# A two-layer sequence model on one core: the first MLP's down projection for sequence 1 by a seven-product scheme, gate and up results in one place, less filler beside the values

## The chip, the cores and the metric

The kernel runs on one core of one Trainium2 chip. The metric is device microseconds of that core for one execution. In this text PE is the matrix engine, DVE the vector engine, ACT the scalar engine, POOL the general engine (GpSimd), and SP the engine whose queue issues nearly all DMAs. Each engine works off its own instructions in order and waits for the others by semaphores.

## The reference, cut to what matters

Two sequences of 1024 tokens with 512 features pass through two layers. Each layer is `x = x + attention(layernorm(x))` and then `x = x + mlp(layernorm(x))`. Everything is 32-bit floating point.

- Layer 0: a gated delta rule (a recurrence with 6 heads of 64), and then MLP 0, with 4096 hidden units, whose weights come as 4-bit codes with scales:

```python
gate = jnp.einsum('td,nd->tn', xt, Wg)
up   = jnp.einsum('td,nd->tn', xt, Wu)
inter = gelu_tanh(gate) * up
out  = jnp.einsum('tn,hn->th', inter, Wd)
```

- Layer 1: attention with 16 heads through a small latent (scores by a softmax over 1024 keys, then the values), and then MLP 1, with 2048 hidden units, in which of every four neighbouring hidden units the two largest are kept.

## The kernel before, in words

**The order of the work.** Before a stage in the middle begins, sequence 0 has gone through layer 0, and MLP 0's weights have been unpacked once and kept in HBM (`kept`). This text is about the stage that follows. Two generators run in it, woven together by `weave` (L158): the main one, `first()` (L1873), is layer 1's attention for sequence 0 (`Latent.run`, L1243) and then its norms; the filler, `Second.run` (L1148), is MLP 0 for sequence 1. Each main step yields the microseconds of filler that it wants beside it, each filler step yields what it is worth, and `weave` adds up and takes filler steps until the debt is paid. So the two lists are written out once, in Python, and the order of PE, DVE and ACT is exactly the program's order (`manual_schedule`, L1862). The order of POOL and of SP's queue is set by the framework's planner from its own idea of durations.

**The main one.** After a stage that makes the keys (14 steps), each half of the queries has a score stage and a value stage. A score step (L1335) has 4 short matmuls on separate row groups of PE and two DVE maxima over 128x1024 (L1349); every eighth step POOL also turns a query (L1232, L1233), which PE then transposes (L1240). In the first score stage `Factors.make` (L1678) uses POOL, DVE and SP as well, to prepare sums of MLP 1's weights. A value step (L1393) has 4 matmuls `st_ps` (L1398), two exponentials of 128x1024 on ACT (L1408), 4 matmuls `av_ps` (L1416); each second one has 4 POOL additions of neighbouring exponentials (`pair`, L1430), and the matmuls `den_ps` (L1437) over the sums that POOL made two steps earlier. The kernel gives 3.4 as the wish of both kinds of step (`per_score`, `per_value`).

**The filler.** MLP 0 for sequence 1 goes over 8 chunks `c` of 512 hidden units. A chunk has two pairs of 2x128 units, and each pair a gate and an up product, in all four "units". A unit is a 256 x 512 by 512 x 1024 product that is done by Strassen's scheme in Winograd's form: seven products of half sizes (table `SEVEN`, L212) instead of eight, with sums of the weights before them (`left_sums`, L223, four POOL operations on 128x256, L226 to L229, over tile `z_raw` that a DMA loads), sums of the tokens (`right_sums`, L233, four DVE operations on 128x1024, once, by `tokens`, L948), and sums behind them. The products take turns on two PSUM banks in the order 1, 2, 6, 5, 7, 3, 4; ACT copies three of them out (`part`, L969), DVE adds the copy and the bank (L1014 in `gate`, L1029 in `up`), ACT applies the GELU to the gate's result `g`, and POOL multiplies (L1030) into `h`. One product is a step of 1.7 (`STEP / 2`), two matmuls with 512 columns.

The down projection of a chunk (L1168 to L1176) is plain: for each of 8 token tiles, four matmuls of 512 columns into `o_ps` (issued at L202), one DVE addition into the tile's `x` (L1173), and a step of 3.4. In the last chunk the tile is stored to HBM at once (L1175). The chunk's weights `wd` (1 MB) are loaded at its start (L1154).

A matmul of 32-bit operands is two records in the profile, so a chunk's down projection is 64 records.

**Elsewhere.** `Sevens` (L1716), at the end of the kernel, is MLP 1 for sequence 1; it has its down projection (L1747) by seven products already, with matmuls of 256 columns (L1758), and shares `gate`, `up`, `part` and `step` with `Second`.

Of the kernel before, what the change touches and what calls it, by code (L numbers as in the profile page):

```python
# [27 lines left out]
F32 = mybir.dt.float32  # L28
# [9 lines left out]
P = 128  # L38
B, T, DM = 2, 1024, 512
# [193 lines left out]
def right_sums(eng, b, new):  # L233

    t2, t3, t4 = new[-3:]
    t1 = new[0] if len(new) == 4 else b["12"]
    if len(new) == 3:
        eng.tensor_sub(t3, b["22"], b["12"])
    eng.tensor_sub(t1, b["12"], b["11"])
    eng.tensor_sub(t2, b["22"], t1)  # L240
    if len(new) == 4:
        eng.tensor_sub(t3, b["22"], b["12"])
    eng.tensor_sub(t4, b["21"], t2)
    return {"11": b["11"], "21": b["21"], "22": b["22"], "T1": t1, "T2": t2, "T3": t3, "T4": t4}
# [695 lines left out]
class Seven:  # L940
# [7 lines left out]
    def tokens(self, xT, pool, eng):  # L948

        half = T // 2  # L950
        blocks = {
            f"{i + 1}{j + 1}": xT[:, 2 * i : 2 * i + 2, j * half : (j + 1) * half] for i in range(2) for j in range(2)
        }
        self.right = right_sums(eng, blocks, [pool.tile([P, 2, half], F32, name=f"xt{i}") for i in range(1, 5)])
# [63 lines left out]
    def up(self, left, g, h):  # L1018
# [3 lines left out]
        for p, ps in self.units(left):  # L1022
            if p in (1, 6, 5):
                parts[p] = self.part(ps)
            elif p == 4:
                nc.vector.tensor_mul(h[:, 1, 0], g[:, 1, 0], ps)
            else:
                i, j, other = {2: (0, 0, 1), 7: (1, 1, 5), 3: (0, 1, 6)}[p]
                nc.vector.tensor_add(h[:, i, j], ps, parts[other])  # L1029
                self.soon.append(lambda v=h[:, i, j], w=g[:, i, j]: self.multiplier.tensor_mul(v, v, w))  # L1030
            yield p

# [93 lines left out]
class Second(Seven):  # L1126
# [3 lines left out]
    def __init__(self, core, banks, xT, kept, park):  # L1130
        super().__init__(core, banks, AF.Gelu_apprx_tanh, core.nc.gpsimd)
        self.kept, self.park = kept, park
# [14 lines left out]

    def run(self):  # L1148
# [3 lines left out]
        for c in range(NC0):  # L1152
            wd = self.wp.tile([P, 4, DM], F32, tag="wd", name="wd")
            nc.sync.dma_start(out=wd, in_=self.kept[2][c])  # L1154
            hs = []
            for pair in range(2):
                g = self.tmp.tile([P, 2, 2, T // 2], F32, tag="g", name="g")
                h = self.wp.tile([P, 2, 2, T // 2], F32, tag=f"h{pair}", name="h0")
                hs.append(h.rearrange("p j m t -> p j (m t)"))
                for w in ("gate", "up"):  # L1160
# [4 lines left out]
                    for p in self.gate(left, g) if w == "gate" else self.up(left, g, h):  # L1165
                        self.step(p, 0)
                        yield STEP / 2
            for t in range(TT):  # L1168
                n = TT + t
                tok = slice(t * P, (t + 1) * P)  # L1170
                po = self.banks.one("o_ps")
                product(nc, po, [(hs[j // 2][:, j % 2, tok], wd[:, j, :]) for j in range(4)])
                nc.vector.tensor_add(core.x[n], core.x[n], po)  # L1173
                if c + 1 == NC0:
                    nc.sync.dma_start(out=self.park[n], in_=core.x[n])  # L1175
                yield STEP  # L1176
# [539 lines left out]
class Sevens(Seven):  # L1716
# [30 lines left out]
    def down(self, c, right, n):  # L1747

        nc = self.core.nc
        dm = DM // 2  # L1750
        for q in range(2):
            self.need((c, q))
            left = self.left[c, q]

            def multiply(ps, l, r, first):
                for i in range(2):
                    for k in range(2):
                        nc.tensor.matmul(  # L1758
                            ps[:, i * dm : (i + 1) * dm],
                            left[l][:, k, i * P : (i + 1) * P],  # L1760
                            right[r][k],
                            start=(first and i == 0 and k == 0),
                            stop=(k == 1),
                            skip_group_check=True,
                        )

            at = [[self.x[:, 4 * m + 2 * q : 4 * m + 2 * q + 2, v * dm : (v + 1) * dm] for v in range(2)] for m in range(2)]
            parts = {}
            for p, ps in self.products(multiply):
                if p in (1, 6, 5):  # L1770
# [207 lines left out]
```

## Time and profile before

| | us |
|---|---|
| median of 3 timed runs (lowest to highest) | 3300.68 (3300.08 to 3304.23) |
| the profiled execution's own time | 3295.47 |
| its span, from the first to the last instruction | 3293.4 |
| PE busy in the span | 3171.5 (96%) |
| DVE busy | 1674.2 (51%) |
| ACT busy | 870.6 (26%) |
| POOL busy | 801.1 (24%) |

Busy time of PE is modelled at its ends, since matmuls are pipelined: the distance from one matmul's start to the next one's is the safer measure of what it costs. A matmul's mean duration (some 0.6 us for 512 columns) is its latency, not its distance. "Idle before" in a row is the time in which an engine had nothing running before the instruction, with the event that ended it. The stage in question goes from 1333 us to 2285 us of the span: the key stage begins it, then come scores (from 1418), values (1600), scores (1790), values (1970), and from 2195 the output projection and the norms. The eight down projections begin at 1410, 1517, 1638, 1775, 1899, 2000, 2136 and 2251 us.

### The profile page before, as it was taken

How to read it: one execution, taken by the hardware profiler on the slowest of the kernel's cores; microseconds unless marked ns; L12 is line 12 of the kernel's file. 1: busy time of each engine (PE TensorE's matmuls, PEld its weight loads, DVE VectorE, ACT ScalarE, POOL GpSimd, SP SyncE). 2: the span in 40 equal slices, each digit the busy share in tenths (PEclk: the TensorE clock that was granted, in tenths of full speed). 3: DMA queues.
4: the chain of work that ended last, by engine and by line, in shares of the span. 5: the costliest groups of instructions: out<-in, count | busy, mean ns of one | idle time of the engine just before them, and what ended most of it. 6: DMA issues, size and time to landing. Idle time of an engine off the chain costs nothing.

```text
span 3293.4 us, 34780 instructions
## 1 busy us (share of the span) xinstructions
PE 3171.5 (96%) x12916; PEld 1567.7 (48%) x12916; DVE 1674.2 (51%) x3317; ACT 870.6 (26%) x1224; POOL 801.1 (24%) x870
## 2 busy tenths in 40 slices
PE   7999899999999999998999999999999999999998
PEld 5777754555555554533333333334433233324547
DVE  6887752445544542456222562123575267433766
ACT  4544311111111110210444113621212610342221
POOL 3433102111111101245545114531100810360000
PEclk9999899999999999999999999999999999999999
DMA  2111234222222212245101100014000010005211
GB/s 88 34 28 30 63 93 139 76 77 71 83 59 70 78 47 93 81 144 173 64 20 35 55 33 26 26 48 135 29 26 13 1 61 10 13 25 169 79 45 48
DMA packets 208201, 204.96 MB, mean 62 GB/s; under 512 B 52960, under 2 KB 172256, under 8 KB 206624
## 3 DMA queue, kind: packets, MB, share of 16 engines
q1 hardware_dynamic: 206592, 197.94, 19.6%
q10 hardware_dynamic: 1440, 4.80, 0.4%
q8 instruction: 102, 1.67, 0.2%
q14 instruction: 67, 0.55, 0.1%
HBM read 141.57 MB, written 61.08 MB: 62 GB/s over the span
## 4 chain that ended last, share of the span: by engine, by line
PE 84%; DVE 8%; ACT 2%; DMA 2%; POOL 2%; issue 1%; SPq 1%; DVEq 0%; POOLq 0%; ACTq 0%
PE o_ps L202 18%; PE z_ps L996 16%; PE u_ps L202 10%; PE g_ps L202 10%; PE st_ps L1398 4%; PE s_ps L1340 4%; PE av_ps L1416 3%; PE z_ps L1758 3%; PE den_ps L1437 2%; PE proj_ps L202 2%; DVE cv L463 1%; PE out_ps L202 1%; PE wide_ps L634 1%; DVE rd L1450 1%; PE small_ps L624 1%
## 5 line engine op out<-in xcount | busy, mean ns | idle before, releaser
L1430 POOL TENSOR_TENSOR es<-es 128x512 f32<-128x512 f32 x256 | 317.9, 1271 | 273.1 <-ACT es L1408 203.8
L1349 DVE TENSOR_REDUCE top<-s_ps 128x2 f32<-128x1024 f32 x256 | 301.2, 1218 | 71.4 <-PE s_ps L1340 71.1
L1408 ACT ACTIVATE es<-st_ps 128x1024 f32<-128x1024 f32 x256 | 248.5, 1021 | 240.8 <-PE st_ps L1398 235.4
L202 PE MATMUL o_ps<-wd,h 128*128 128x512 f32 x512 | 236.8, 605 | 2.0 <-POOL h L1030 2.0
L202 PE MATMUL g_ps<-xT,w_gate 128*128 128x512 f32 x512 | 233.1, 597 | 1.3 <-DVE h L935 1.3
L202 PE MATMUL u_ps<-xT,w_up 128*128 128x512 f32 x512 | 232.1, 596 | 1.8 <-ACT gelu L930 1.8
L202 PE MATMUL o_ps<-w_down,h 128*128 128x512 f32 x512 | 228.6, 597 | 0.7 <-DVE h L935 0.5
L969 ACT COPY part<-z_ps 128x512 f32<-128x512 f32 x168 | 98.1, 584 | 453.1 <-PE z_ps L996 354.5
L1398 PE MATMUL st_ps<-q,kT 17*128 17x512 f32 x1024 | 174.5, 640 | 4.2 <-ACT es L1408 1.1
L935 DVE TENSOR_TENSOR h<-gelu,u_ps 128x512 f32<-128x512 f32 x64 | 44.0, 687 | 249.0 <-PE u_ps L202 249.0
L1340 PE MATMUL s_ps<-kT,q 16*128 16x512 f32 x1024 | 153.1, 643 | 3.9 <-DVE top L1349 3.9
L202 PEld LDWEIGHTS o_ps<-wd,h 128*128 128x128 f32 x512 | 92.7, 191 | 134.6 <-issue 126.4
L202 PEld LDWEIGHTS u_ps<-xT,w_up 128*128 128x128 f32 x512 | 94.6, 190 | 109.8 <-issue 104.3
L202 PEld LDWEIGHTS o_ps<-w_down,h 128*128 128x128 f32 x512 | 94.6, 190 | 109.4 <-issue 105.0
L202 PEld LDWEIGHTS g_ps<-xT,w_gate 128*128 128x128 f32 x512 | 94.1, 190 | 107.7 <-issue 103.6
L202 PE MATMUL proj_ps<-xT,wqkv 128*128 128x256 f32 x576 | 132.9, 385 | 11.3 <-ACT gw L421 10.1
L1173 DVE TENSOR_TENSOR x<-x,o_ps 128x512 f32<-128x512 f32 x64 | 44.0, 687 | 193.4 <-PE o_ps L202 193.4
L930 ACT ACTIVATE gelu<-g_ps 128x512 f32<-128x512 f32 x64 | 38.2, 597 | 388.4 <-PE g_ps L202 369.4
L1416 PE MATMUL av_ps<-es,v 128*32 128x512 f32 x1024 | 136.3, 604 | 0.0
L996 PE MATMUL z_ps<-xt,z_raw 128*128 128x512 f32 x256 | 122.2, 600 | 0.0
L202 PEld LDWEIGHTS proj_ps<-xT,wqkv 128*128 128x128 f32 x576 | 107.5, 191 | 29.2 <-ACT gw L421 12.3
L996 PE MATMUL z_ps<-xt,z_sum 128*128 128x512 f32 x256 | 119.5, 601 | 0.8 <-DVE g L1014 0.8
(279 smaller groups left out, 5081.3 us busy)
## 6 DMA issues: line engine op xcount, KB each, us to landing
sums<-factor SPq DMA_DIRECT2D x24, 512.0 KB, 3.1
kept_gate<-w_gate SPq DMA_DIRECT2D x16, 512.0 KB, 3.5
kept_up<-w_up SPq DMA_DIRECT2D x16, 512.0 KB, 3.5
kept_down<-w_down SPq DMA_DIRECT2D x16, 512.0 KB, 3.1
z_raw<-kept_gate SPq DMA_DIRECT2D x16, 512.0 KB, 3.7
z_raw<-kept_up SPq DMA_DIRECT2D x16, 512.0 KB, 3.7
wd<-kept_down SPq DMA_DIRECT2D x8, 1024.0 KB, 4.8
xl<-park SPq DMA_DIRECT2D x32, 256.0 KB, 2.8
```

Source lines behind the costliest of these rows:

```text
L202: nc.tensor.matmul(ps, lhsT, rhs, start=(i == 0), stop=(i == len(pairs) - 1))
L935: nc.vector.tensor_mul(h, gl, pu)
L969: self.core.nc.scalar.copy(t, src)
L996: self.core.nc.tensor.matmul(ps, left[l][:, k, :], self.right[r][:, k, :], start=(first and k == 0), stop=(k == 1), skip_group_check=True,)
L1340: nc.tensor.matmul(tiles[h4 // 2][:, h4 % 2 * 512 : h4 % 2 * 512 + 512], q1s[t][r : r + HALF, gr, :], kT[r : r + HALF, gr, j * 512 : (j + ...
L1349: nc.vector.tensor_reduce(top[:, j, h : h + 2], tiles[e].rearrange("p (i k) -> p i k", i=2), AX.X, ALU.max, negate=True)
L1398: nc.tensor.matmul(tiles[h4 // 2][:, h4 % 2 * 512 : h4 % 2 * 512 + 512], kT[r : r + CR, gr, kt * P : (kt + 1) * P], q2[r : r + CR, gr, :], ...
L1408: nc.scalar.activation(t.rearrange("p i q -> p (i q)"), tiles[e], AF.Exp, scale=HALF**-0.5)
L1416: nc.tensor.matmul(av[gr][32 * h4 : 32 * h4 + 32, :], v[:, kt, 4 * gr + h4, :], es[u][h4 // 2][:, h4 % 2, :], start=(kt == 0), stop=(kt == ...
L1430: nc.gpsimd.tensor_add(t, t, es[u][h4 // 2][:, h4 % 2, :])
L1437: nc.tensor.matmul(den[gr][32 * h4 : 32 * h4 + 32, :], self.ones, es[u - 1][h4 // 2][:, h4 % 2, :], start=(kt == 1), stop=(kt == TT - 1),)
L1758: nc.tensor.matmul(ps[:, i * dm : (i + 1) * dm], left[l][:, k, i * P : (i + 1) * P], right[r][k], start=(first and i == 0 and k == 0), sto ...
```

## The change

- `Second`'s down projection is done by the seven products too. `down_weights` loads `wd` and makes its four sums on POOL, on 128x512 each. Token halves are the row blocks; the tokens are taken in two parts `q`, each of 2 x 256 tokens. For each part DVE makes four sums of the hidden results (`left`, on 128x512), which are issued behind product 1; product 6 is the first to use them. A product is 4 matmuls of 256 columns. ACT copies products 1, 6 and 5 out, DVE adds products 2, 7, 3 and 4 from PSUM into `x`, and POOL adds the three copies into `x`. One product is a step of 1.7.
- The last chunk's stores of `x` all stand behind its last product.
- Gate and up share one place: the gate's result is written where the hidden result will be, the up result stays in the tile `part`, and POOL (in `Sevens`, DVE) multiplies in place. The tile `g` is gone; a `part` is held until that multiplication.
- The sums of the tokens, of `Second` and of `Sevens`, overwrite one block of `xT`, and the sum T3 is made ahead of T1 and T2 instead of behind them.
- `x` of sequence 1 is one tile with 8 slices instead of 8 tiles.
- `per_value` of this stage's attention is 3.0 instead of 3.4.
- `Sevens` calls the same function for its down projection (`output`), with DVE as before.

```diff
 def right_sums(eng, b, new):
-    t2, t3, t4 = new[-3:]
-    t1 = new[0] if len(new) == 4 else b["12"]
-    if len(new) == 3:
-        eng.tensor_sub(t3, b["22"], b["12"])
-    eng.tensor_sub(t1, b["12"], b["11"])
-    eng.tensor_sub(t2, b["22"], t1)
-    if len(new) == 4:
-        eng.tensor_sub(t3, b["22"], b["12"])
+    t2, t3, t4 = new
+    eng.tensor_sub(t3, b["22"], b["12"])
+    eng.tensor_sub(b["12"], b["12"], b["11"])
+    eng.tensor_sub(t2, b["22"], b["12"])
     eng.tensor_sub(t4, b["21"], t2)
...
-    def up(self, left, g, h):
+    def up(self, left, g):
...
             elif p == 4:
-                nc.vector.tensor_mul(h[:, 1, 0], g[:, 1, 0], ps)
+                nc.vector.tensor_mul(g[:, 1, 0], g[:, 1, 0], ps)
             else:
                 i, j, other = {2: (0, 0, 1), 7: (1, 1, 5), 3: (0, 1, 6)}[p]
-                nc.vector.tensor_add(h[:, i, j], ps, parts[other])
-                self.soon.append(lambda v=h[:, i, j], w=g[:, i, j]: self.multiplier.tensor_mul(v, v, w))
+                v = parts[other]
+                nc.vector.tensor_add(v, ps, v)
+                self.soon.append(lambda w=g[:, i, j], v=v: self.multiplier.tensor_mul(w, w, v))
             yield p
+
+    def output(self, left, right, at, adder):
+        nc, dm = self.core.nc, DM // 2
+        def multiply(ps, l, r, first):
+            for i in range(2):
+                for k in range(2):
+                    nc.tensor.matmul(
+                        ps[:, i * dm : (i + 1) * dm],
+                        left[l][:, k, i * P : (i + 1) * P],
+                        right[r][k],
+                        start=(first and i == 0 and k == 0),
+                        stop=(k == 1),
+                        skip_group_check=True,
+                    )
+        parts = {}
+        for p, ps in self.products(multiply):
+            if p in (1, 6, 5):
+                parts[p] = self.part(ps).rearrange("p (i d) -> p i d", i=2)
+            else:
+                x = {2: at[0][0], 7: at[1][1], 3: at[0][1], 4: at[1][0]}[p]
+                nc.vector.tensor_add(x, x, ps.rearrange("p (i d) -> p i d", i=2))
+                if p != 4:
+                    self.soon.append(lambda x=x, v=parts[{2: 1, 7: 5, 3: 6}[p]]: adder.tensor_add(x, x, v))
+            yield p
...
 class Second(Seven):
+    def down_weights(self, c):
+        wd = self.wp.tile([P, 4, DM], F32, tag="wd", name="wd")
+        self.core.nc.sync.dma_start(out=wd, in_=self.kept[2][c])
+        half = DM // 2
+        blocks = {
+            f"{i + 1}{j + 1}": wd[:, 2 * i : 2 * i + 2, j * half : (j + 1) * half] for i in range(2) for j in range(2)
+        }
+        new = [self.wp.tile([P, 2, half], F32, name=f"wd_t{i}") for i in range(2, 5)]
+        right = right_sums(self.core.nc.gpsimd, blocks, new)
+        return {name: [t[:, k, :] for k in range(2)] for name, t in right.items()}
+
+    def left(self, hs, q, calls):
+        blocks = {
+            f"{i + 1}{j + 1}": hs[j][:, :, i, q * HB : (q + 1) * HB] for i in range(2) for j in range(2)
+        }
+        new = [self.wp.tile([P, 2, HB], F32, name=f"h_s{i}") for i in (1, 2, 4)]
+        return left_sums(Recorder(self.core.nc.vector, calls), blocks, new)
 
     def run(self):
...
-            wd = self.wp.tile([P, 4, DM], F32, tag="wd", name="wd")
-            nc.sync.dma_start(out=wd, in_=self.kept[2][c])
+            right = self.down_weights(c)
...
-                g = self.tmp.tile([P, 2, 2, T // 2], F32, tag="g", name="g")
-                h = self.wp.tile([P, 2, 2, T // 2], F32, tag=f"h{pair}", name="h0")
-                hs.append(h.rearrange("p j m t -> p j (m t)"))
+                g = self.wp.tile([P, 2, 2, T // 2], F32, tag=f"h{pair}", name="h0")
+                hs.append(g)
...
-            for t in range(TT):
-                n = TT + t
-                tok = slice(t * P, (t + 1) * P)
-                po = self.banks.one("o_ps")
-                product(nc, po, [(hs[j // 2][:, j % 2, tok], wd[:, j, :]) for j in range(4)])
-                nc.vector.tensor_add(core.x[n], core.x[n], po)
-                if c + 1 == NC0:
+            calls = deque()
+            lefts = [self.left(hs, 0, calls)]
+            for q in range(2):
+                for p in self.output(lefts[q], right, self.places(self.x, q), nc.gpsimd):
+                    self.step(p, 0)
+                    if q == 0 and p == 1:
+                        while calls:
+                            calls.popleft()()
+                    if q == 0 and p == 4:
+                        lefts.append(self.left(hs, 1, calls))
+                    if q == 1 and p == 1:
+                        while calls:
+                            calls.popleft()()
+                    yield STEP / 2
+            if c + 1 == NC0:
+                self.step(4, 0)
+                for n in range(TT, NT):
                     nc.sync.dma_start(out=self.park[n], in_=core.x[n])
-                yield STEP
...
-            yield from att.run(0, "right", parks[0], parks[1], 3.4, 3.4, False, beside=factors.make)
+            yield from att.run(0, "right", parks[0], parks[1], 3.4, 3.0, False, beside=factors.make)
```

## The prediction

> **What bounds the kernel now.** I read the page's busy times first, then the busy time of each engine by stage of the stretch in question, then who made PE wait there, then single rows in order of time. By stage (columns: us of the stretch, then PE, PE's weight loads, DVE, ACT, POOL busy with their counts, granted clock, DMA share, GB/s):
>
> ```profile
> 1340.00:1418.00 78.00, 78.00 (x281) 41.25 (x279) 30.24 (x70) 24.12 (x42) 31.06 (x48) 1.00 0.22 65
> 1418.00:1600.00 182.00, 171.33 (x584) 67.17 (x584) 112.53 (x136) 23.02 (x40) 79.95 (x109) 0.97 0.48 159
> 1600.00:1790.00 190.00, 187.88 (x849) 62.45 (x848) 40.70 (x58) 100.56 (x110) 105.26 (x97) 1.00 0.07 23
> 1790.00:1970.00 180.00, 180.00 (x617) 68.99 (x615) 104.07 (x116) 24.07 (x39) 32.09 (x40) 1.00 0.13 44
> 1970.00:2165.00 195.00, 193.27 (x837) 66.44 (x836) 45.69 (x66) 88.76 (x100) 101.04 (x95) 1.00 0.08 25
> 2165.00:2285.00 120.00, 120.00 (x370) 51.13 (x369) 37.97 (x74) 26.55 (x38) 25.27 (x28) 1.00 0.35 113
> ```
>
> PE is without a gap in four of six stages; DVE is at most 62% busy, ACT 53%, POOL 55%. The whole stretch has two PE waits over 1 us, both in the first score stage:
>
> ```profile
> PE hT_ps L1240 <- POOL n L1233: 8.7, 1, 8.7
> PE o_ps L202 <- POOL h L1030: 2.0, 1, 2.0
> ```
>
> Both are POOL being late, held by a weight load before it in its queue. So PE's own work sets the time here: what it sheds is gained, except where another engine begins to hold it. POOL is the one that has done so.
>
> **What PE sheds.** The price is the distance of starts (PE rows in time, at the stretch's end and in MLP 1's down projection, which has the new form):
>
> ```profile
> 2250.61 3.60 PE L202 MATMUL o_ps<-wd,h 128*128 128x512 f32 x8
> 2254.04 0.60 PE L150 MATMUL ln_ps<-ident,ln_xn 128*128 128x128 f32 x4
> ...
> 3208.89 3.62 PE L1758 MATMUL z_ps<-z_right,z_h 128*128 128x256 f32 x16
> 3212.35 3.62 PE L1758 MATMUL z_ps<-z_right,z_hsum 128*128 128x256 f32 x16
> 3215.80 1.89 PE L1758 MATMUL z_ps<-z_right,z_h 128*128 128x256 f32 x8
> 3217.53 1.89 PE L1758 MATMUL z_ps<-z_right,z_hsum 128*128 128x256 f32 x8
> 3223.21 2.07 PE L1758 MATMUL z_ps<-z_right,z_h 128*128 128x256 f32 x4 [3.79 <-DVE x_last L1774]
> ```
>
> Eight records of 512 columns take 3.43 us (0.429 each); sixteen of 256 take 3.46, or 3.45 (0.216 each). A chunk had 8 token tiles x 3.43 = 27.4 us and gets 14 products x 1.73 = 24.2. Eight chunks: 8 x 3.2 = **26 us less** on the path. PE's changes between main work and filler stay: there are as many main steps as before.
>
> **The lists stay matched.** The main one's wishes were 176 x 3.4 = 598.4 (99 steps at `per_score` or norms, 77 at `per_value`), the filler's worth 8 x (28 x 1.7 + 8 x 3.4) = 598.4. Now it is 99 x 3.4 + 77 x 3.0 = 567.6 against 8 x 42 x 1.7 = 571.2: two products are left over at the end and run alone. So less filler beside the values costs nothing by itself, and a shortage of filler isn't to be expected.
>
> **What is added, and its cover.**
>
> 1. DVE: 8 sums per chunk at 0.69 (as the addition of 128x512 from SBUF, L1777, 0.686), 5.5 us per chunk of over 100; the 8 additions of 0.687 into `x` were there before. In a score step PE takes 4.7 us, and DVE 2.4 for the maxima and some 0.8 for additions; four sums in a row (2.75) are absorbed in two steps. They stand behind a POOL multiplication (L1030); behind the sums on DVE stand product 2's addition and the next maxima. Product 6 needs the second sum some 3 to 6 us after issue. From 0 to 1 us per chunk; I take 0, since the old form needed the same multiplication at once and lost 2.0 us in all.
> 2. ACT: 6 copies of 0.584 per chunk, where it had only exponentials. In a value step it idles 4 us during a down projection. 0.
> 3. The two banks now turn over every 1.73 us, not 3.43. The units run that way already, with no PE wait beyond those above. In MLP 1 the new form lost the 3.79 us above behind DVE, which there also compares hidden units. Between 0 and 112 x 0.07 = 8 us (3.8 us over 56 products there); I take 1, nearer the units.
> 4. POOL, per chunk: 4 sums of `wd` at 1.27 (L1430's shape) and 6 additions into `x` at 1.27: 12.7 us. In the value stages that is 55% going to some 70%. As a total it is covered; by moments see below.
> 5. T3 first, at the start: product 6 began at 1336.41, right behind T2's end, so T2 later by one operation costs 1.2 us:
>
> ```profile
> 1333.78 1.22 DVE L239 TENSOR_TENSOR xt<-xT 128x1024 f32<-128x1024 f32 x1
> 1335.04 1.23 DVE L240 TENSOR_TENSOR xt<-xT,xt 128x1024 f32<-128x1024 f32 x1
> ```
>
>    In `Sevens` the first product waits for a DMA and the order is hidden.
> 6. The last stores: all behind the last product. SP issues them in order (0.33 each) and the next attention's loads after; the first load lands some 6.5 us after the last product (1.3 addition, 2.4 issues, 2.8 landing). DVE then measures it and must have it ready for a transpose about 10.3 us after (three matmul groups of 3.43). 0 to 4; I take 1.
> 7. One place for gate and up: as many operations, other operands: 0. A `part` is held until POOL's multiplication; with 4 buffers ACT would wait only if POOL were over 8 us late.
>
> **Filler beside the values.** 70 value steps now take 210 / 1.7 = 123.5 products, so some 16 steps have one product instead of two: PE needs 6.56 - 1.81 = 4.75 us with `den_ps` and 3.9 without. ACT in a gate unit beside values (rows in time):
>
> ```profile
> 1706.09 1.94 ACT L1408 ACTIVATE es<-st_ps 128x1024 f32<-128x1024 f32 x2
> 1708.05 1.28 ACT L1011 ACT_TABLE_LOAD   x1
> 1709.34 0.60 ACT L1011 ACTIVATE g<-z_ps 128x512 f32<-128x512 f32 x1
> 1709.83 0.62 ACT L1015 ACTIVATE g<-g 128x512 f32<-128x512 f32 x1
> ```
>
> With the second table load ACT needs 1.94 + 2.56 + 0.63 = 5.1 us per step. A third of the filler is gate units, so 5 steps lack 0.4 to 1.2 us: 0 to 6 us; I take 1, since ACT catches up in the next steps.
>
> The skill speaks against such steps. The Trainium skill, "ScalarE: Activation LUTs", section "What ACT_TABLE_LOAD costs", puts every switch of tables at some 2.66 us, 1.28 for the load and 1.38 for a drain. By that an ACT step would be an estimated 7.9 us, over even the old two-product step, and the five steps would lose some 18 us. The row shows the load of 1.28 with the activation beginning 0.01 behind it, so the trace decides for 5.1.
>
> **POOL by moments.** At each chunk's start but the first, POOL meets the four sums of `wd` (5.1 us), whose load can only begin near the end of the chunk before and takes 4.8, and then a `z_sum` group (2.9). That is up to 12.8 us in which the main one's POOL work may be queued behind. A value step's additions have this slack:
>
> ```profile
> 1707.19 5.06 POOL L1430 TENSOR_TENSOR es<-es 128x512 f32<-128x512 f32 x4 [8.60 <-ACT es L1408]
> 1717.76 1.04 PE L1437 MATMUL den_ps<-es,ones 128*32 128x512 f32 x8
> ```
>
> 1717.76 - 1712.25 = 5.5 us. So a start beside values (three of them, by the wishes) costs 0 to 12.8 - 5.5 = 7.3, and a start beside scores (four) costs 0 to the 8.7 that a late turned query cost. Bounds 0 to 57. I take 4 in all: the planner mostly puts work whose input is there first, and twenty-odd waits of POOL for `z_raw` cost PE 10.7. Below nothing: those 10.7 may go, since everything shifts.
>
> **Sum.** -26 + 1 (banks) + 1.2 (T2) + 1 (stores) + 1 (ACT) + 4 (POOL) = **-18 us**. Of the profiled execution: span 3293.4 to 3275, own time 3295.5 to 3277.5. The median of the timed runs is 5.2 above that execution; from 3300.7 I forecast **3283**.
>
> **Rivals.**
>
> - **Nothing new waits**, and the old POOL waits shrink: -26 - 5 + 1 gives 3271. For it: no gap on PE in the second score stage, 45% of POOL free. Against: POOL did hold PE once.
> - **Half is given back on the banks and in DVE.** Copies, sums and maxima meet, and a product of 1.73 us is a short cover: 8 us (item 3) + 8 x 1 (item 1) leaves -26 + 16 = -10: 3291. For it: the 3.79 above. Against: there DVE adds the copies too, and here POOL does.
> - **POOL takes PE's place: slower.** At each of the seven later starts the additions or the query wait behind `wd`'s load and sums. From 33 us on, 4.7 per start, the kernel is slower by over 0.2%; at the bounds, 57 us, it ends at 3300.7 - 26 + 57 = 3332. I put the case at 3312. For it: in-order POOL, 8.7 us once; after that wait the granted clock dipped as well (0.97 in the stage). Against: the load lands some 3 us into the chunk, and slack is 5.5.
> - **The scheme does nothing here**, because the smaller matmuls cost as much: excluded by 0.216 against 0.429, unless weight loads (0.19 each) show up between main steps. 3300, little chance.
>
> **Chances.** Forecast (3277 to 3290) 0.46; nothing waits 0.24; half given back 0.16; POOL slower 0.09; nothing gained 0.05. A measurement here tells 0.2% (6.6 us) from no change. Half of the "half" case lies over 3294.1. Faster by more: 0.46 + 0.24 + 0.08 = 0.78; within: 0.08 + 0.05 = 0.13; slower: 0.09. The range leaves out the slower case and the best tail: 3267 to 3299.
>
> **What would show it.** Right: rows of L202 `o_ps<-wd` gone, 896 records of 256 columns at a distance of 0.216; PE's waits in the stretch under 20 us; the stretch some 18 us shorter, all else alike. POOL wrong: `den_ps` or `hT_ps` waiting for POOL with several us each at chunk starts. Banks wrong: PE waiting for ACT `part` or DVE `x` in the new products. ACT wrong: `st_ps` waiting for `es` in gate units. The prediction fails if one cause comes back at most starts.

## The result and the profile after

The changed kernel takes 3293.3 us (median of 22 runs, 3284.5 to 3302.4), where the kernel before took 3300.8 beside it (22 runs, 3292.1 to 3309.5): a ratio of 0.9979, with a 95% interval of 0.9969 to 0.9989, or 7.5 us less. The forecast was 3283, 18 less. Two executions that ran much longer at a lower granted clock, one of `e16_all_three` (4051.9 us) and one of the kernel before in the last round (3397.4 us), are left out of the medians and ratios in this text. Its profiled execution took 3296.5, with a span of 3294.8.

The stage in question is measured below from the first product of `Second` to the first gate-score matmul of MLP 1 behind it. It took 948.6 us before and 947.3 after. By stage, in the columns of the prediction's table (keys, scores, values, scores, values, output and norms; line numbers are now those of the changed kernel):

```profile
1338.00:1416.00 78.00, 78.00 (x296) 44.29 (x295) 33.38 (x76) 26.39 (x46) 32.50 (x49) 1.00 0.22 65
1416.00:1617.00 201.00, 180.73 (x681) 89.71 (x680) 126.89 (x150) 30.18 (x52) 109.56 (x133) 0.93 0.45 144
1617.00:1798.00 181.00, 177.16 (x896) 71.75 (x895) 47.53 (x68) 94.21 (x108) 116.74 (x104) 1.00 0.07 24
1798.00:1978.00 180.00, 179.04 (x706) 86.28 (x705) 114.12 (x130) 29.93 (x49) 58.73 (x60) 1.00 0.14 47
1978.00:2163.00 185.00, 182.02 (x893) 76.92 (x892) 56.42 (x76) 93.33 (x108) 116.34 (x106) 1.00 0.07 23
2163.00:2282.00 119.00, 118.83 (x452) 66.42 (x451) 46.50 (x84) 31.65 (x47) 43.75 (x41) 1.00 0.29 100
```

One row stands out. The first score stage is 19 us longer than before (201 for 182), PE is idle in it for 20 us where it was idle for 11, and its granted clock fell from 0.97 to 0.93. The windows of the value stages are 9 and 10 us shorter, because they hold less filler. The rows are windows of time, not the stages' exact edges. The last three edges between rows, here and in the prediction's table, are 18 to 30 us early (so are the 1790 and 1970 under "Time and profile before"): by the first score and value matmuls, the second score stage runs from 1816.4 to 2001.9 (before: 1810.0 to 1993.6). Cut so, the first score stage takes 201.5 us for 182.6, the first value stage 198.4 for 209.4, and the second score stage 185.5 for 183.6, so the reading is the same. PE's waits from 1340 us on, the five longest rows (engine, line, waited for: us, times, longest):

```profile
PE hT_ps L1299 <- POOL n L1292: 10.2, 2, 10.0
PE den_ps L1496 <- DVE rd L1509: 6.8, 6, 1.3
PE z_ps L992 <- DVE h L1010: 6.2, 1, 6.2
PE z_ps L1038 <- DVE h_s L1772: 2.5, 1, 2.5
PE z_ps L1038 <- DVE x L1053: 1.7, 2, 1.3
```

The three largest single waits (10.0, 6.2, 2.5) are all in the first score stage. PE's new products cost what the forecast said; two neighbours in the norms, 8 records each, start 1.73 us apart:

```profile
2255.56 1.89 PE L1038 MATMUL z_ps<-wd_t,h_s 128*128 128x256 f32 x8
2257.29 1.89 PE L1038 MATMUL z_ps<-wd,h_s 128*128 128x256 f32 x8
```

Counted from each matmul's start to the next one's, the down projection fell from 233.5 us to 208.4 in the stage: 25.1 less. So the saving came, and some 24 us were given back in the same stage, nearly half of them in the intervals behind the score matmuls (`s_ps`, 78.3 to 89.9).

How the row comes about shows in two queues, POOL's and SP's, in time (start, us, engine, line; in brackets the idle time before and what ended it):

```profile
1443.65 1.26 POOL L1055 TENSOR_TENSOR x<-x,part 128x512 f32<-128x512 f32 x1
1451.85 1.27 POOL L236 TENSOR_TENSOR wd_t<-wd 128x512 f32<-128x512 f32 x1 [6.95 <-DMA wd<-kept_down]
...
1457.18 0.72 POOL L1733 TENSOR_TENSOR factor<-factor 128x256 f32<-128x256 f32 x1
...
1473.97 0.72 POOL L226 TENSOR_TENSOR z_sum<-z_raw 128x256 f32<-128x256 f32 x1 [10.42 <-DMA z_raw<-kept_up]
...
1492.83 0.72 POOL L226 TENSOR_TENSOR z_sum<-z_raw 128x256 f32<-128x256 f32 x1 [8.01 <-DMA z_raw<-kept_gate]
...
1496.08 0.45 POOL L1292 TENSOR_TENSOR n<-rot_c,rot_s 128x128 f32<-128x128 f32 x1
```

```profile
1444.63 0.36 SPq L1747 DMA_DIRECT2D sums<-factor  x1
1453.08 1.92 SPq L1716 DMA_DIRECT2D factor<-in_w_gate  x4
1459.30 0.34 SPq L1747 DMA_DIRECT2D sums<-factor  x1
1461.97 1.91 SPq L1716 DMA_DIRECT2D factor<-in_w_up  x4
1463.98 0.40 SPq L1747 DMA_DIRECT2D sums<-factor  x1
1467.11 1.91 SPq L1716 DMA_DIRECT2D factor<-in_w_gate  x4
1469.12 0.53 SPq L955 DMA_DIRECT2D z_raw<-kept_up  x1
```

POOL waits 6.95 us for `wd`, with factor sums queued behind it. SP's next store of a factor sum can go only at 1459.30, when POOL has made one; the next factor loads wait for stores to land, and the load of `z_raw` stands behind both and leaves at 1469.12. So POOL, with nothing else at the head of its queue, waits 10.42 us for `z_raw`, meets the same loop again, and turns the query (`n`) so late that PE waits 10 us. So the theory was a jam of two in-order queues that wait for each other. The experiments test it against the rival that POOL's or DVE's new work as such, or the banks, take the time.

### The profile page after: what moved, and what is told of

Its sections match the earlier page's. It is cut to its first block, busy times and chain, and to the rows that moved or that the text cites. A ratio compares the mean times of both kernels' runs of the same rounds, so it can differ in the third digit from the quotient of the medians.

```text
span 3294.8 us, 35848 instructions
## 1 busy us (share of the span) xinstructions
PE 3160.3 (96%) x13300; PEld 1646.5 (50%) x13300; DVE 1729.0 (52%) x3381; ACT 888.0 (27%) x1264; POOL 909.6 (28%) x950
## 4 chain that ended last, share of the span: by engine, by line
PE 81%; DVE 9%; DMA 2%; POOL 2%; ACT 2%; issue 2%; SPq 1%; DVEq 0%; POOLq 0%; ACTq 0%
PE z_ps L992 16%; PE o_ps L202 11%; PE u_ps L202 10%; PE g_ps L202 10%; PE z_ps L1038 8%; PE st_ps L1457 4%; PE s_ps L1399 4%; PE av_ps L1475 3%; PE den_ps L1496 2%; PE proj_ps L202 2%; DVE cv L459 1%; PE out_ps L202 1%; DVE rd L1509 1%; PE wide_ps L630 1%; PE small_ps L620 1%
## 5 line engine op out<-in xcount | busy, mean ns | idle before, releaser
L965 ACT COPY part<-z_ps 128x512 f32<-128x512 f32 x216 | 126.4, 585 | 582.8 <-PE z_ps L992 363.5
L1026 DVE TENSOR_TENSOR part<-z_ps,part 128x512 f32<-128x512 f32 x72 | 49.7, 690 | 160.4 <-PE z_ps L992 154.6
L992 PE MATMUL z_ps<-xT,z_left 128*128 128x512 f32 x256 | 120.2, 602 | 3.2 <-DMA z_left<-in_w_gate 3.1
L992 PE MATMUL z_ps<-xT,z_sum 128*128 128x512 f32 x256 | 122.5, 601 | 0.0
L118 POOL TENSOR_TENSOR ln_rs<-ln_rs,nhalf 128x1 f32<-128x1 f32 x64 | 35.7, 559 | 310.9 <-DVE ln_rs L117 310.7
```

The lines of the kernel that those rows point to most:

```text
L965: self.core.nc.scalar.copy(t, src)
L992: self.core.nc.tensor.matmul(ps, left[l][:, k, :], self.right[r][:, k, :], start=(first and k == 0), stop=(k == 1), skip_group_check=True,)
L1026: nc.vector.tensor_add(v, ps, v)
```

## The experiments

All are edits of the changed kernel unless said otherwise. Ratios are to the kernel before on the same chip, with 95% intervals; "stage" is from the kernel's profile, and "half clock" the time at a granted clock of 0.5 in it. Each stage is read from one profile. In three profiles of the changed kernel (at the end of this section) it scatters by 2.5 us, so a difference of that size between two rows says nothing.

| kernel | median us | ratio | stage | half clock |
|---|---|---|---|---|
| before | 3300.8 | 1 | 948.6 | 10.2 |
| after | 3293.3 | 0.9979 (0.9969 to 0.9989) | 947.3 | 27.3 |
| e1_late_wd_sums | 3291.0 | 0.9980 (0.9968 to 0.9992) | 947.0 | 27.3 |
| e2_factors_on_dve | 3287.3 | 0.9960 (0.9944 to 0.9977) | 939.9 | 20.5 |
| e3_wish_34 | 3300.2 | 1.0010 (1.0000 to 1.0021) | 948.8 | 33.5 |
| e4_plain_down | 3297.1 | 1.0002 (0.9989 to 1.0016) | 948.4 | 10.2 |
| e7_after_no_factors | 3262.4 | 0.9881 (0.9864 to 0.9898) | 915.5 | 0 |
| e8_before_no_factors | 3283.9 | 0.9949 (0.9931 to 0.9967) | 936.2 | 0 |
| e9_wd_sums_on_dve | 3285.6 | 0.9963 (0.9947 to 0.9979) | 938.3 | 17.1 |
| e6_weights_on_act_queue | 3274.9 | 0.9928 (0.9913 to 0.9943) | 932.6 | 17.1 |
| e12_before_act_queue | 3286.0 | 0.9964 (0.9953 to 0.9976) | 936.3 | 0 |
| e13_sum_stores_on_pool | 3289.0 | 0.9966 (0.9955 to 0.9977) | 941.5 | 20.5 |
| e14_act_queue_wd_dve | 3273.1 | 0.9929 (0.9913 to 0.9945) | 927.0 | 6.8 |
| e16_all_three | 3273.9 | 0.9924 (0.9905 to 0.9942) | 926.9 | 6.8 |
| e17_three_and_x_on_dve | 3279.0 | 0.9937 (0.9918 to 0.9956) | 931.4 | 10.2 |
| e11_both_dve_act_queue | 3284.1 | 0.9949 (0.9930 to 0.9968) | 928.2 | 3.4 |

**One part alone.** First, the wish of a value step back at 3.4:

```diff
-            yield from att.run(0, "right", parks[0], parks[1], 3.4, 3.0, False, beside=factors.make)
+            yield from att.run(0, "right", parks[0], parks[1], 3.4, 3.4, False, beside=factors.make)
```

> The changed kernel with the value steps' wish back at 3.4. The main one then wants 598.4 and the filler has 571.2, so some 27 of filler are missing at the end and the output projection and the norms run with 8 of their 14 steps bare. Theory of the prediction (less filler is only the balance of the lists): the value stages lose nothing, their PE waits for DVE's reciprocals fall back from 6.8 to 4 us, and the end is longer, since bare steps wait for DVE and ACT: 3 to 15 us over the changed kernel, 3296 to 3308. Rival (steps with one product are what costs): faster than the changed kernel by some 5 us, 3288.

It lost all of the gain. The filler ran out before the norms, whose transposes then waited alone:

```profile
PE ln_ps L150 <- DVE ln_xn L142: 10.5, 8, 1.7
...
PE den_ps L1496 <- DVE rd L1509: 3.6, 4, 0.9
```

So the wish of 3.0 is needed for the balance of the lists, and it has a price: `den_ps` waits 6.8 us for `rd` with it, 3.6 without. Then the plain down projection of before, with that wish, and all else of the change (the shared place, T3 first, `x` as one tile):

```diff
-                for p in self.output(lefts[q], right, self.places(self.x, q), nc.gpsimd):
...
+                product(nc, po, [(hs[j // 2][:, j % 2, tok], wd[:, j, :]) for j in range(4)])
+                nc.vector.tensor_add(core.x[n], core.x[n], po)
```

> The changed kernel with the down projection of the kernel before (plain, eight token tiles) and the wish of 3.4, so that of the change only the shared place of gate and up, the sums of the tokens in place with T3 first, and x as one tile are left. If these cost nothing, as I predicted but for T3 (1.2 us), it is the kernel before, 3300 to 3303. If holding a part until POOL's multiplication costs ACT, or writing the gate's result over the hidden tile costs PE, it is slower, 3306 or more, and a part of what the change gave back is here.

The ratio is 1.0002: these parts neither cost nor gain anything that can be measured.

**The sums of `wd` later, on POOL:**

```diff
-        right = right_sums(self.core.nc.gpsimd, blocks, new)
...
+        right = right_sums(Recorder(self.core.nc.gpsimd, calls), blocks, new)
...
+                while pair and sums:
+                    sums.popleft()()
```

> The changed kernel with POOL's four sums of wd issued 14 products later, behind the first pair of units, when their load has long landed. Theory A (POOL stands in its queue behind the load of wd, and what is behind it, the weight sums of MLP 1, their stores on SP and the loads behind those, comes late, until PE waits): the 7 us waits of POOL for wd go, PE's waits in the first score stage fall from some 20 us by 6 to 12, and the time is 6 to 12 us under the changed kernel, about 3284. Theory B (POOL's added work as such, 12.7 us a chunk, is what holds PE, wherever it stands): no change, 3293. Theory C (the waits are those of the stage before the change, moved about by chance): no change in the mean, with the waits in other places.

This one tells nothing. The planner, which orders POOL, put the sums where they had been, and the wait stayed:

```profile
POOL wd_t L1775 <- DMA wd<-kept_down: 13.4, 2, 6.8
```

**All factor sums on DVE:**

```diff
-        first, rest = self.core.nc.vector, self.core.nc.gpsimd
+        first, rest = self.core.nc.vector, self.core.nc.vector
```

> The changed kernel with all four sums of each of MLP 1's weight blocks (Factors.add) on DVE, none on POOL: some 50 us less on POOL and 24 x 3 x 0.41 = 30 us more on DVE in the first score stage. Theory A (what is lost there is the coupling of POOL's queue, the stores of sums on SP and the weight loads behind them): the 10 us wait of hT_ps for POOL and the 6 us wait behind DVE go, and with them the half clock that follows; 12 to 18 us under the changed kernel, about 3278 to 3281. Theory B (DVE's own load in the score steps is what delays): DVE gets worse, the time is that of the changed kernel or above, 3293 to 3300.

The stage fell by 7.4 us, and the wait for `n` from 10.0 to 5.6: what POOL does for MLP 1 has a part in the loss, but a smaller one than the 12 to 18 us that theory A expected. The next pair asks how large a part the meeting with it has in all.

**Without the weight sums of MLP 1**, in the changed kernel and in the one before. Both leave out the making of these sums and load a slice of `w1_gate` where a sum would be read (shown for the changed kernel; the one before has the wish 3.4):

```diff
-        self.core.nc.sync.dma_start(out=t[:, 3:, :], in_=self.sums[u])
+        self.core.nc.sync.dma_start(out=t[:, 3:, :], in_=self.a["w1_gate"][u[0]][:, :, : 2 * P])
...
-            yield from att.run(0, "right", parks[0], parks[1], 3.4, 3.0, False, beside=factors.make)
+            yield from att.run(0, "right", parks[0], parks[1], 3.4, 3.0, False)
```

> The change, with the making of MLP 1's weight sums beside the first score stage left out (its part Factors.make is not run; at their use a slice of w1_gate of the same shape is loaded in place of each sum, so this part of the computation is left out). To be read with its twin, the kernel before with the same cut. Theory (the loss is a jam of POOL and SP in the first score stage, where the factor sums and their transfers meet the new sums of wd): the waits on n (10.1 us), on h (6.3), on h_s (2.6) and the half-clock stretches go, the stage from the first z_ps to the first sgate comes to 920 to 930 us, and this kernel is 20 to 27 us faster than its twin. Rival (POOL's own new work, the banks and DVE take it, whatever Factors does): the waits stay and the difference to the twin is 5 to 12 us, as between after and before.

> The kernel before, with the making of MLP 1's weight sums beside the first score stage left out as in its twin (that part of the computation is left out). Theory of the jam: before pays for it too (8.8 us on n, 2.1 on POOL's h), so this is 5 to 15 us faster than before, and its stage 935 to 945 us against 948.6. Rival (Factors cost nothing but their DVE sum): within 5 us of before.

Here the theory's number came: the twins differ by 21.5 us in their medians (the two ratios divided give 0.9932, some 0.991 to 0.996) and by 20.7 in the stage. (The changed twin's stage, 915.5, lies under the 920 to 930 expected.) PE's waits behind 1340 us in the changed twin, and then in the twin of before:

```profile
PE den_ps L1496 <- DVE rd L1509: 6.8, 6, 1.3
PE z_ps L1038 <- DVE x L1053: 0.4, 1, 0.4
PE s_ps L1399 <- DVE top L1408: 0.2, 1, 0.2
PE hT_ps L1299 <- POOL n L1292: 0.2, 1, 0.2
```

```profile
PE den_ps L1437 <- DVE rd L1450: 4.2, 4, 1.6
PE hT_ps L1240 <- POOL n L1233: 0.2, 1, 0.2
```

The waits for `n`, `h` and `h_s` are gone, and PE's first score stage has no gap and a clock of 1.00 (the changed twin, same columns as the stages above; the row ends ahead of the stage's last steps, and the whole stage takes 170.5 us, 169.8 in the twin of before):

```profile
1419.00:1572.00 153.00, 153.00 (x638) 77.21 (x638) 106.40 (x119) 26.76 (x46) 52.06 (x55) 1.00 0.09 31
```

So the jam costs 947.3 - 915.5 = 31.8 us with the change and 948.6 - 936.2 = 12.4 without it. The change made it 19.4 us dearer (18.5 by the means of three profiles of each kernel). Of the 31.8 us some 21 are PE's waits (28.4 for 7.6 in the twin) and some 9, an estimate from the distances of starts, are matmuls at the granted clock of 0.5. POOL's and DVE's new work, the quicker turn of the banks and the smaller wish, with no jam, cost 5 us in all: PE sheds 25.7 us and the stage falls by 20.7. This pair does not say which of the many things that it leaves out was the cause: POOL and DVE work, SP's queue and the traffic went together. The next ones do.

**The loads of `z_raw` from ACT's queue**, in the changed kernel and in the one before:

```diff
-        self.core.nc.sync.dma_start(out=t, in_=src)
+        self.core.nc.scalar.dma_start(out=t, in_=src)
```

> The change, with the loads of the gate and up weights (z_raw) issued by ACT instead of SP. If what makes the weight sums late is SP's queue (the stores of factor sums wait there for POOL, with the z_raw loads behind them), POOL's waits for z_raw of 8 to 10 us shrink, and with them the wait on n and on h: 3283 to 3290. If it is POOL's own order that is late, or ACT's issue time delays exp and the part copies, nothing is gained: 3292 to 3300.

> The kernel before, with the loads of the gate and up weights (z_raw) issued by ACT instead of SP: the twin of the change with the same move. Theory (the change was worth its full amount and gave two thirds of it back to a jam behind SP's queue that it makes worse): before has the jam in small (12.4 us of its stage, by its twin without the weight sums of MLP 1), so the move takes 5 to 12 us from it, 3289 to 3296, and the change is worth 15 to 21 us on top of it. Rival (the move of the loads is worth some 18 us by itself, whatever the down projection does): 3280 to 3286, and the change stays at 6 to 12 us.

One line takes 14.7 us from the stage with the change, more than expected, and 12.3 from the stage before: there it is the whole jam. The three longest rows that are left with the change, and all that is left before:

```profile
PE den_ps L1496 <- DVE rd L1509: 6.8, 6, 1.3
PE z_ps L992 <- DVE h L1010: 6.8, 1, 6.8
PE z_ps L992 <- ACT part L965: 2.1, 1, 2.1
```

```profile
PE den_ps L1437 <- DVE rd L1450: 3.9, 4, 1.3
PE hT_ps L1240 <- POOL n L1233: 0.2, 1, 0.2
```

The wait for `n` went in both, as the theory has it: the place of these loads in SP's queue made it. The move has a second side that these runs don't part from the first: in SP's queue a load of `z_raw` can itself stand waiting until PE has freed a buffer (26.0 us in three waits between 1400 and 1620 us with the change, 68.7 in seven before), and whatever of the factor sums' stores and loads comes next stands behind it. And the 15 to 21 us that the theory expected of the change on top of the move did not come: 11 us by the medians (the two ratios divided: 0.9964, some 0.9945 to 0.9983), 3.7 in the stage, because with the change 17 us of the jam remain. One part of that is seen on DVE, where a factor sum stands at the head of the queue waiting for its load, with `h` behind it:

```profile
1569.70 0.82 DVE L1726 TENSOR_TENSOR factor<-factor 128x256 f32<-128x256 f32 x1 [7.59 <-DMA factor<-in_w_down]
1570.44 1.28 DVE L1010 TENSOR_TENSOR h<-z_ps,part 128x512 f32<-128x512 f32 x2
```

By the medians it is the rival on record that came true, at the edge of its range: 3286.0 before (it had 3280 to 3286), and the change still worth 11 us (it had 6 to 12). So what the place of these loads in SP's queue costs was for the most part there before the change (12.3 us of the stage, 14.7 with it), and is not what the change made dearer.

**The sums of `wd` on DVE**, whose order the program keeps, 14 products after the chunk's start; alone, and with the move of the loads:

```diff
-        right = right_sums(self.core.nc.gpsimd, blocks, new)
...
+        right = right_sums(Recorder(self.core.nc.vector, calls), blocks, new)
...
+                while pair and sums:
+                    sums.popleft()()
```

> The change, with the four sums of each chunk's down weights on DVE, 14 products after the chunk's start, where DVE's order is kept as written. Theory of the jam: POOL no longer waits for wd (13 to 14 us in the score stage of after) and has 8 x 5.1 us less to do, so the waits on n and h shrink from 16.4 us to under 8 and the kernel is 4 to 10 us faster than after, 3284 to 3290. Rival (DVE is the engine that is late): DVE's 8 x 2.7 us come on top of its queue, the waits on rd, x and h grow, 3293 to 3300.

> The change with two moves together: the z_raw loads issued by ACT, and the four sums of the down weights on DVE 14 products later. If the two remove different waits (SP's queue; POOL's 12.5 us wait for wd), they add up: 6 to 9 us less than the change with the loads on ACT alone, 3266 to 3270. If they remove the same jam, nothing is added: 3272 to 3278.

Alone it takes 9.0 us from the stage (the wait for `n` falls from 10.0 to 6.0), on top of the move 5.6. So POOL's sums of `wd` are the change's own entry into the jam. Whether that is POOL's wait for their load or the work itself, some 5 us a chunk, is not parted: this edit takes both from POOL, and e1, which should have moved the wait alone, did not move it. The medians of the two kernels with the move (3274.9 and 3273.1) don't tell the 5.6 apart, and they lie outside the 3266 to 3270 that was expected.

**The stores of factor sums issued by POOL**, alone and with both moves:

```diff
-            self.core.nc.sync.dma_start(out=self.sums[u], in_=ts.pop(u)[:, 3:, :])
+            self.core.nc.gpsimd.dma_start(out=self.sums[u], in_=ts.pop(u)[:, 3:, :])
```

> The change, with the stores of MLP 1's weight sums issued by POOL, which makes the sums, instead of SP; the z_raw loads stay on SP. If SP's waits for those sums (42 us in all in the first score stage of after) hold the loads behind them, this takes most of the jam away from the other side: the wait on n under 5 us and 3278 to 3288. If the sums' place in POOL's own order is what is late, or POOL's issue costs as much, the same waits stay: 3289 to 3297.

> The change with three moves: z_raw loads issued by ACT, the sums of the down weights on DVE 14 products later, the stores of MLP 1's weight sums issued by POOL. What is left in the change with the loads on ACT is one wait of 6.9 us on h, behind a DVE sum that waits for its factor load, which stands on SP behind a store. If the stores free SP, that goes too: 3258 to 3266, the time of the change without the weight sums (3262). If POOL's issue time or its order makes a new wait: 3268 to 3280.

Alone it takes 5.8 us from the stage and leaves the wait for `n` at 7.3, between the two expectations; with the other two it adds nothing (926.9 against 927.0). So the stores on SP seem to be one link of the loop, and not the only one; the run's ratio does not differ clearly from the change's (0.9955 to 0.9977 against 0.9969 to 0.9989).

**What is left.** Two runs on the remaining 927.0 - 915.5 = 11.5 us; the first adds the x additions to DVE (`adder` is `nc.vector` in `output`), the second the factor sums:

> The change with the z_raw loads issued by ACT, the sums of the down weights on DVE, and the additions of a part to x on DVE instead of POOL (48 x 1.27 us off POOL, 48 x 0.7 on DVE). Of the jam's 31.8 us in the first score stage 11.5 are left with the first two moves. If they are POOL's busy time, the stage falls from 927 to 918 to 923 and the time to 3264 to 3270. If they are transfers and DVE's queue, DVE's new work adds waits on x: 3273 to 3280.

> The change with the z_raw loads issued by ACT, and both the sums of the down weights and all of MLP 1's weight sums on DVE, so that POOL makes only the sums of z_raw, the multiplications and the rotations. If the rest of the jam is the exchange of factor sums between DVE and POOL (POOL waited 22 and 4.5 us for DVE's first sum with the first two moves), the stage falls from 927 to 918 to 923, 3264 to 3269. If DVE is now the late one (its waits for factor loads stand ahead of h and part), 927 to 940 and 3273 to 3286.

Neither closes the rest: 931.4 and 928.2. In the second, work taken from POOL comes back as small waits on DVE (`h` 3.1 us, `x` 1.9, `part` 1.2). In the kernel with the first two moves, PE's waits are some 5 us longer than in the changed twin (the longest 2.8, for ACT's `part`), and 6.8 us at the granted clock of 0.5 cost some 3 more; the rest is spread over distances of starts. What causes these 11.5 us is not settled. So of the 19.4 us that the change added to the jam, 5.6 to 9.0 go with POOL's sums of `wd`, the place of the `z_raw` loads takes 2.4 more than before, and over half stays open.

**Where the medians' 7.5 us lie**, when the stage shows 1.3: both kernels, unchanged, profiled twice more.

> The kernel before, unchanged, for a second profile of it. In the profiles at hand the stage with the change is 1.3 us shorter than before, while the medians differ by 7.5. If the stage repeats to within 1 us (948 to 949.5), the rest of the 7.5 us lies outside it, and the parts ahead of it and behind it differ between kernels or scatter. If the stage itself varies from execution to execution by several us, the one pair of profiles is not enough.

> The change, unchanged, for a second profile of it. If the stage repeats (946.5 to 948) and the ratio is again 0.997 to 0.999, 2 to 8 us of the gain lie outside the stage: then the part ahead of it should be shorter than before's in both pairs of profiles. If it is scatter, the parts ahead and behind differ as much between two profiles of one kernel as between the kernels.

> The kernel before once more, a third profile, on the same question: stage 948 to 949.5 if it repeats; the part ahead of the stage 1333 to 1340 if that belongs to the kernel, anywhere from 1326 to 1340 if it scatters.

> The change once more, a third profile, on the same question: stage 946.5 to 948 if it repeats; the part ahead of the stage 1326 to 1334 if that belongs to the kernel, anywhere from 1326 to 1340 if it scatters.

The stage repeats: 948.6, 948.5, 948.4 before, and 947.3, 944.8, 946.8 after, 2.2 less on the mean. The part ahead of it scatters (1333.0, 1328.9, 1327.6 before; 1331.2, 1334.6, 1329.2 after), and so does the part behind (1011.8, 1019.3, 1018.9; 1016.3, 1016.1, 1012.8), in neither kernel's favour. The wait for `n` comes back in all three profiles after (10.0, 9.8, 9.9), the wait for `h` is of no fixed size (6.2, 3.8, 2.5). In this round the ratios were 0.9988 (0.9975 to 1.0001) and 0.9986 (0.9973 to 0.9998), some 4 us. So the change is worth 2 us in the stage by the profiles, and 4 to 7 us by the medians; what lies between is not assigned to any step.

## Why the prediction was wrong, point by point

- **What PE sheds, 26 us: right.** 25.1 with the jam, 25.7 between the twins (230.0 to 204.3), and 0.216 a record. The rival "nothing gained" is out.
- **The rest of the way, without the jam:** the stage of the twins comes near the forecast's other terms: -25.7, +3.0 at the values, +0.9 at the scores, +0.6 in the units, +0.5 at `st_ps`: -20.7. The forecast's sum without its 4 for POOL is -21.8.
- **DVE sums 0, banks 1, ACT copies 0, one place 0:** right, the four together. Without the jam PE waits 0.4 us for `x` and none for `h_s` or `part`; e4 shows the shared place at nothing.
- **T2, 1.2:** half right. PE waits 1.1 us for T2 at the start, but a wait of 0.8 for `g` three microseconds later went for it.
- **Last stores, 1:** no wait of PE for them in any profile.
- **Filler beside the values, 1 (bounds 0 to 6), on ACT:** inside its bounds, wrong engine. `st_ps` waits for no exponential; what came is `den_ps` waiting for DVE's `rd`, 3 us more, and e3 shows that it is the wish. A wait of 1.3 us of this kind stood in the profile before already; the prediction's "two PE waits over 1 us" left it out.
- **POOL by moments, 4 (bounds 0 to 57): the step that failed.** By the twins, the meeting with MLP 1's factor sums cost 19.4, inside the bounds. I priced POOL's meeting with `wd` at each start by itself and trusted the planner to put "work whose input is there first". It put the sums of `wd`, for which POOL stood 6.95 us, ahead of a factor sum whose input DVE had ready at 1450.30, 1.55 us before the load of `wd` released POOL, in the one stage where MLP 1's factor sums share POOL and SP; there a late POOL makes its own next input late, as the two queues show. How much of the 19.4 comes through this loop stays open: the moves of loads and sums account for 8 of them. At the five later starts outside that stage PE waits for POOL nowhere. I had the first wait (8.7 us on `n`) in the profile and had put it down to POOL held by a weight load; I did not follow the load back to SP, whose queue was waiting for POOL. POOL's and then SP's rows of before show the same loop, a factor store that can go when POOL has made the sum (1522.72), a factor load that waits for the store, and the load of `z_raw` behind both:

```profile
1516.35 0.73 POOL L226 TENSOR_TENSOR z_sum<-z_raw 128x256 f32<-128x256 f32 x1 [11.60 <-DMA z_raw<-kept_up]
...
1521.78 0.91 POOL L1676 TENSOR_TENSOR factor<-factor 128x256 f32<-128x256 f32 x1
...
1533.05 0.72 POOL L226 TENSOR_TENSOR z_sum<-z_raw 128x256 f32<-128x256 f32 x1 [5.86 <-DMA z_raw<-kept_gate]
...
1522.72 0.33 SPq L1688 DMA_DIRECT2D sums<-factor  x1
1525.33 1.75 SPq L1651 DMA_DIRECT2D factor<-in_w_down  x4
...
1527.66 0.53 SPq L959 DMA_DIRECT2D z_raw<-kept_gate  x1
```

- **What bounds the kernel:** PE is without a gap in three of the six rows of the prediction's table, not four. The step above does not rest on it.
- **The rivals.** "Half given back on the banks and in DVE" had the nearest time, 3291, but by luck: the twins refute its reason. "POOL takes PE's place" had the engine, but not the place: one stage, not seven starts. That "nothing new waits" would give 3271 is what the move of the loads reached (3274.9), 12 us of which the kernel before could have had too.

The version that beats both kernels is the change with the loads on ACT's queue: a ratio of 0.9928 to before, some 24 us less, with the one line; the sums of `wd` on DVE as well (0.9929) shorten the stage, but not measurably the whole.

## What to carry to other kernels

When PE's work shrinks and the gain does not come, look for the stage that grew and follow its longest wait back through each queue until it returns to an engine already passed. An operation added to such a loop of two in-order queues can cost more than its own time and its own wait. A wait in the profile of before, behind a transfer that was issued late, is a warning that new waits on that engine may not come alone (here the jam went from 12.4 us to 31.8). Test it by leaving the neighbour out of both kernels, and by moving one load to another queue; an edit in a program whose order a planner sets has to be looked up in the trace before its time is read.

## What the runs showed of the hardware

The granted clock fell in the middle of a busy kernel, behind single waits. Around the end of the wait of 10.0 us it was 0.50 for 10.2 us (first row), and around that of 6.2 us for as long (third row); behind that of 2.5 us it was 0.5 for 3.4 us, from 1532.0 (second row, of which it fills three quarters). The columns are those of the stages:

```profile
1491.00:1501.20 10.20, 4.61 (x9) 2.55 (x10) 0.23 (x1) 0.58 (x1) 8.29 (x13) 0.50 0.25 92
1531.00:1535.00 4.00, 3.69 (x10) 3.04 (x11) 4.00 (x6) 0.48 (x1) 0.17 (x1) 0.62 0.82 251
1583.20:1593.40 10.20, 5.83 (x7) 2.52 (x8) 3.88 (x5) 1.74 (x3) 4.67 (x8) 0.50 0.49 182
...
1549.00:1552.40 3.40, 3.40 (x8) 2.71 (x9) 3.37 (x4) 0.00 (x0) 3.24 (x4) 0.50 0.87 298
```

The last row is a fourth stretch, behind a wait of only 1.3 us (for `x`, ended at 1548.9). Waits as long for `rd` in the value stages (1.3 us, from 1682.0, 1729.3 and 1776.6) had none behind them, so the length of a single wait does not tell whether the clock falls. In the stage after, this cost PE some 8 to 9 us, against some 1.5 before: an estimate from the distances of starts in such stretches. The Trainium skill, "TensorE: Matmul & The Clock Gate", section "HAM oscillation — how this bites in real kernels", warns of gaps over some 3.4 us; the long waits agree, and the stretches behind waits of 2.5 and 1.3 us show that the clock can fall behind shorter ones.

Three profiles of the kernel before differ by up to 7.5 us in the parts outside the woven stage (1327.6 to 1333.0 ahead of it, 1011.8 to 1019.3 behind it), while the woven stage repeats within 0.2 us before and 2.5 after. So the length of a stage, even from one profile each, seems to tell apart effects of 5 us that medians of six executions do not (932.6 and 927.0 against 3274.9 and 3273.1).
